# Chunks of 512 with spread preparation in a Mamba layer, and a second top-p attention whose search runs in three parts over three row tiles

## The chip, the cores and the metric

The kernel runs on one core of one Trainium2 chip. The metric is the device time of one execution in microseconds (us). All runs named here were in the fast state, and every kernel was timed beside the kernel before on the same chip. PE is TensorE, DVE is VectorE, ACT is ScalarE, POOL is GpSimd.

## The reference, cut to what matters

Four layers, each `x = layernorm(x + layer(x, adj))`, on x of 3327 rows (padded to 26 tiles of 128) by 256, fp32. The change touches layer 1 and layer 3.

```python
# layer 1: graph convolution, layer norm, Mamba (512 channels, 16 states)
h = relu(adj @ x @ gcn_w + gcn_b);  h = layernorm(h) * ln_g + ln_b
xc, z = split(h @ w_in)
u = silu(causal_conv4(xc));  dbc = u @ w_xp;  dt = softplus(dbc[:, :16] @ w_dt + b_dt)
B, C = dbc[:, 16:32], dbc[:, 32:]
hst[t] = exp(dt[t] * A) * hst[t-1] + dt[t] * B[t] * u[t]      # for each of 16 states
y = (hst @ C + u * D_skip) * silu(z);  out = y @ w_out

# layer 3: two steps; in each
probs = softmax((Xa @ W1.T @ W2.T) @ (Xa @ W3.T).T)
# keep the largest entries of a row until their sum reaches 0.9; equal entries by lower index first
A = probs * mask;  A = A / A.sum(-1)
Xf = R @ Xf;  Xa = A @ Xa;  Z = Z + Xf @ U1[n].T + Xa @ U2[n].T
```

In the first attention a row keeps few entries, in the second many. The second search therefore guesses a threshold c1, sums what lies over it, moves to c2, sums again, fits c3 a little below the cut, and ranks exactly only what lies under c3.

## The kernel before

Layer 1. `pump()` issues one step of the graph convolution's stream: six products, or the last two of a tile and its tail (nine products a step in the changed kernel). `head(c)` prepares a chunk of 384 columns, and all of it is issued after state 9 of the chunk before; `tail(c)` ends a chunk.

```python
            def head(c):

                w = min(WC, npad - c * WC)
                xc = scratch("xc")
                nc.vector.tensor_copy(xc[:, :, :3], last)
                u = ch.tile([P, NG, WC], F32, name="u")[:, :, :w]
                for g in range(NG):
                    nc.scalar.copy(xc[:, g, 3:3 + w], project(c, g, w))
                    ug = u[:, g, :]
                    nc.vector.tensor_scalar(ug, xc[:, g, 0:w], conv_w[:, g, 0:1], conv_b[:, g:g + 1],
                                            op0=ALU.mult, op1=ALU.add)
                    ...  # (three more taps; Silu of u; product with w_xp, copied to dbc: cut)
                e, e1 = scratch("e")[:, :, :w], scratch("e1")[:, :, :w]
                for g in range(NG):
                    ps = psum.tile([P, WC], F32, name="ps")
                    nc.tensor.matmul(ps[:, :w], w_dt[:, g * P:(g + 1) * P], dbc[:DTR, :w],
                                     start=True, stop=True)
                    nc.scalar.activation(dt[:, g, :], ps[:, :w], AF.Identity, bias=b_dt[:, g:g + 1])
                    nc.scalar.activation(e[:, g, :], ps[:, :w], AF.Abs, bias=b_dt[:, g:g + 1])
                nc.scalar.activation(e, e, AF.Exp, scale=-1.0)
                nc.vector.tensor_scalar_add(e1, e, 1.0)
                nc.vector.scalar_tensor_tensor(e, e1, 1.0, e, op0=ALU.subtract, op1=ALU.subtract)
                nc.scalar.activation(e1, e1, AF.Ln)
                nc.vector.tensor_sub(e1, e1, e)
                ...  # (dt = softplus, du = dt * u: cut)
                return u, dbc, dt, du

            def scan(dbc, dt, du, s, ys):
                ...
                for r in (DTR + s, DTR + DS + s):
                    ps = psum.tile([P, WC], F32, name="ps")
                    nc.tensor.matmul(ps[:, :w], ident[:R, r:r + 1].to_broadcast([R, P]), dbc[:, :w],
                                     start=True, stop=True)
                    row = work.tile([P, 1, WC], F32, name="row", bufs=4)
                    nc.scalar.copy(row[:, 0, :w], ps[:, :w])
                    bc.append(row[:, :, :w].to_broadcast([P, NG, w]))
                dA = work.tile([P, NG, WC], F32, name="dA", bufs=2)[:, :, :w]
                for g in range(NG):
                    nc.scalar.activation(dA[:, g, :], dt[:, g, :], AF.Exp, scale=A[:, g, s:s + 1])
                h = work.tile([P, NG, WC], F32, name="h")[:, :, :w]
                nc.vector.tensor_mul(h, du, bc[0])
                for g in range(NG):
                    nc.vector.tensor_tensor_scan(h[:, g, :], dA[:, g, :], h[:, g, :], initial=carry[:, s, g:g + 1],
                                                 op0=ALU.mult, op1=ALU.add)
                nc.vector.tensor_copy(carry[:, s, :], h[:, :, w - 1])
                nc.vector.tensor_mul(h, h, bc[1])
                for g in range(NG):
                    nc.tensor.matmul(ys[g][:, :w], ident, h[:, g, :], start=(s == 0), stop=(s == DS - 1))


            def tail(c, u, ys):

                w = u.shape[2]
                sz, y = scratch("sz")[:, :, :w], scratch("y")[:, :, :w]
                for g in range(NG):
                    nc.scalar.activation(sz[:, g, :], project(c, NG + g, w), AF.Silu)
                for g in range(NG):
                    nc.vector.scalar_tensor_tensor(y[:, g, :], u[:, g, :], d_skip[:, g:g + 1], ys[g][:, :w],
                                                   op0=ALU.mult, op1=ALU.add)
                nc.vector.tensor_mul(y, y, sz)
                nt_c = w // P
                ...  # (product with w_out, residual, layer norm of the chunk: cut)

            tw = WC // P
            pump(tiles=tw + 1)
            nxt = head(0)
            for c in range(nch):
                u, dbc, dt, du = nxt
                ys = [ypsum.tile([P, WC], F32, name=f"y{g}") for g in range(NG)]
                for s in range(DS):
                    scan(dbc, dt, du, s, ys)
                    pump()
                    if s == 9 and c + 1 < nch:
                        pump(tiles=(c + 2) * tw)
                        nxt = head(c + 1)
                tail(c, u, ys)
```

Layer 3. One tile's whole search comes before the attention of the tile before it:

```python
        def search_long(work, e, total, v, kept):
            nc.vector.max(m8, e)                                   # over all 3328 columns
            ...
            nc.scalar.activation(junk, e, AF.Exp, bias=hneg, scale=0.5, accum_out=root)
            exponentials(e, m8[:, 0:1], total)
            ...
            nc.scalar.activation(junk, e, AF.Sign, bias=c1, scale=-1.0, accum_out=sg)
            over(c1, m1)                  # DVE: sum of e where e >= c1
            ...  # k1 from sg; c2 from c1, k1, m1
            over(c2, m2)                  # DVE: sum of e where e >= c2
            ...  # c3 from c2 and the slope between the two sums
            nc.vector.scalar_tensor_tensor(z, e, c3, e, op0=ALU.is_lt, op1=ALU.mult, accum_out=rest)
            top = ranked(work, segment_tops(work, z), RPT)   # 32 segments of 104, top 8 each; 7 rounds
            cs = crossing(work, v, top, 8 * RPT, base, lim)
            ...  # rep: which copies of the value v are kept
            for k in range(0, TIES, 8):   # two replacements over 3328 columns
                nc.vector.match_replace(z, rep[:, k:k + 8], z if k else e, 2.0)
            nc.vector.scalar_tensor_tensor(e, z, v, e, op0=ALU.is_gt, op1=ALU.mult, accum_out=kept)

        # one_pass (es starts with the search of tile 0)
                for it in range(nt):
                    if it + 1 < nt:
                        es.append(ahead(it + 1))      # logits and search of the next tile
                    step(it, work, psum, atp, ...)    # attention of this tile, diffusion, finish
```

Of the kernel before, what the change touches and what calls it, by code (L numbers as in the profile page):

```python
# [22 lines left out]
JS = 6  # L23
WC = 384
# [9 lines left out]
SEG = 104  # L34
RP0, RPT = 6, 7
TIES = 16
UNDER = 24.0
KC = 416
# [3 lines left out]
def gnn_kernel(ctx: ExitStack, tc: tile.TileContext, n: int, a: dict, out: bass.AP):  # L42
# [84 lines left out]
    with tc.tile_pool(name="l01", bufs=1) as xpool:  # L127
# [30 lines left out]
        with tc.tile_pool(name="l1b", bufs=1) as wpool, tc.tile_pool(name="l1aw", bufs=2) as cwork, \  # L158
                tc.tile_pool(name="l1at", bufs=3) as atp, tc.tile_pool(name="l1c", bufs=2) as ch, \
                tc.tile_pool(name="l1t", bufs=4) as tmp, tc.tile_pool(name="l1s", bufs=3) as work, \  # L160
                tc.tile_pool(name="l1p", bufs=2, space=PSUM) as psum, \
# [26 lines left out]
            hTs = {}  # L188

            def scratch(name):  # L190
                return tmp.tile([P, NG, 3 + WC], F32, name="t")

            def convolve():

                for it in range(nt):
                    c, i = divmod(it * P, WC)
                    if i == 0:
                        hTs[c] = ch.tile([P, D // P, WC], F32, name="hT")
                    acc = cpsum.tile([P, D], F32, name="acc")
                    for j in range(nt):  # L200
# [5 lines left out]
                        if j % JS == JS - 1:  # L206
                            yield it
                    m = cwork.tile([P, D], F32, name="m")
                    nc.scalar.copy(m, acc)
                    mt = transposed(cwork, cpsum, m, "mt")  # L210
                    po = cpsum.tile([P, D], F32, name="acc")
                    for k in range(2):
                        nc.tensor.matmul(po, mt[:, k, :], gw[:, k, :], start=(k == 0), stop=False)
                    nc.tensor.matmul(po, one, gb, start=False, stop=True)
                    h = cwork.tile([P, D], F32, name="h")
                    nc.scalar.activation(h, po, AF.Relu)
# [5 lines left out]
                    pt = cpsum.tile([P, D // P, P], F32, name="ps")  # L222
                    for k in range(2):
                        nc.tensor.transpose(pt[:, k, :], h[:, k * P:(k + 1) * P], ident)
                        nc.scalar.activation(hTs[c][:, k, i:i + P], pt[:, k, :], AF.Identity,
                                             scale=g1[:, k:k + 1], bias=b1[:, k:k + 1])
                    yield it + 1
# [20 lines left out]
            def head(c):  # L248

                w = min(WC, npad - c * WC)  # L250
                xc = scratch("xc")
                nc.vector.tensor_copy(xc[:, :, :3], last)
                u = ch.tile([P, NG, WC], F32, name="u")[:, :, :w]
                for g in range(NG):
# [4 lines left out]
                    for k in range(1, 4):  # L259
                        nc.vector.scalar_tensor_tensor(ug, xc[:, g, k:k + w], conv_w[:, g, k:k + 1], ug,  # L260
                                                       op0=ALU.mult, op1=ALU.add)
                nc.vector.tensor_copy(last, xc[:, :, w:w + 3])
                nc.scalar.activation(u, u, AF.Silu)
                ps = psum.tile([P, WC], F32, name="ps")
# [4 lines left out]
                nc.scalar.copy(dbc[:, :w], ps[:R, :w])  # L269


                dt = ch.tile([P, NG, WC], F32, name="dt")[:, :, :w]
                e, e1 = scratch("e")[:, :, :w], scratch("e1")[:, :, :w]
                for g in range(NG):
# [3 lines left out]
                    nc.scalar.activation(dt[:, g, :], ps[:, :w], AF.Identity, bias=b_dt[:, g:g + 1])  # L278
                    nc.scalar.activation(e[:, g, :], ps[:, :w], AF.Abs, bias=b_dt[:, g:g + 1])
                nc.scalar.activation(e, e, AF.Exp, scale=-1.0)  # L280
                nc.vector.tensor_scalar_add(e1, e, 1.0)
                nc.vector.scalar_tensor_tensor(e, e1, 1.0, e, op0=ALU.subtract, op1=ALU.subtract)
                nc.scalar.activation(e1, e1, AF.Ln)
                nc.vector.tensor_sub(e1, e1, e)
                nc.vector.scalar_tensor_tensor(dt, dt, 0.0, e1, op0=ALU.max, op1=ALU.add)
                du = ch.tile([P, NG, WC], F32, name="du")[:, :, :w]
                nc.vector.tensor_mul(du, dt, u)
                return u, dbc, dt, du

            def scan(dbc, dt, du, s, ys):  # L290

                w = dt.shape[2]
                bc = []
                for r in (DTR + s, DTR + DS + s):
# [3 lines left out]
                    row = work.tile([P, 1, WC], F32, name="row", bufs=4)  # L298
                    nc.scalar.copy(row[:, 0, :w], ps[:, :w])  # L299
                    bc.append(row[:, :, :w].to_broadcast([P, NG, w]))  # L300
                dA = work.tile([P, NG, WC], F32, name="dA", bufs=2)[:, :, :w]
                for g in range(NG):
                    nc.scalar.activation(dA[:, g, :], dt[:, g, :], AF.Exp, scale=A[:, g, s:s + 1])  # L303
                h = work.tile([P, NG, WC], F32, name="h")[:, :, :w]
                nc.vector.tensor_mul(h, du, bc[0])  # L305
                for g in range(NG):
                    nc.vector.tensor_tensor_scan(h[:, g, :], dA[:, g, :], h[:, g, :], initial=carry[:, s, g:g + 1],  # L307
                                                 op0=ALU.mult, op1=ALU.add)
                nc.vector.tensor_copy(carry[:, s, :], h[:, :, w - 1])
                nc.vector.tensor_mul(h, h, bc[1])  # L310
                for g in range(NG):
                    nc.tensor.matmul(ys[g][:, :w], ident, h[:, g, :], start=(s == 0), stop=(s == DS - 1))  # L312

            def tail(c, u, ys):

                w = u.shape[2]
                sz, y = scratch("sz")[:, :, :w], scratch("y")[:, :, :w]
# [201 lines left out]
    with tc.tile_pool(name="l3", bufs=1) as pool, tc.tile_pool(name="l3s", bufs=4) as sm:  # L519
# [16 lines left out]
        for k in range(TIES):  # L536
            nc.vector.memset(count[:, k:k + 1], k)
# [402 lines left out]
```

## Time and profile before

| | us |
|---|---|
| median, 4 runs of the rounds with the changed kernel | 4768.2 (4766.3 to 4769.8) |
| layer 0 ends / layer 1 ends / layer 2 ends | 365 / 1942 / 2297 |
| first attention ends / second attention ends | 3240 / 4764 |

The span in 40 equal slices, from the page of the kernel before; a digit is the busy share in tenths, PEclk the granted clock of TensorE in tenths.

```profile
PE   8998888898888877899799999997577776767786
DVE  1111897788787888688245454541888888888886
PEclk9998998898898887999699999996788888888888
```

The two stretches where DVE shows mostly 7 or 8 and PE mostly 6 to 8 (slices 5 to 17 and 29 to 40) are layer 1 from its first scan on and the second attention. Where DVE shows 4 and 5 and PE 9, the kernel is TensorE's. The stretches, waits and groups that the argument rests on stand in the prediction.

### The profile page before, as it was taken

The numbers are of one execution on the slowest core, as the hardware profiler recorded it, in microseconds if no ns is written. First come the engines' busy times: TensorE is split into PE (matmuls) and PEld (weight loads), VectorE is DVE, ScalarE is ACT, GpSimd is POOL, SyncE is SP. The second block draws the span as 40 slices with busy tenths as digits, with TensorE's granted clock in tenths as the row PEclk, the third lists the DMA queues.
The fourth block names the chain that finished last, engine by engine and source line by source line (L and its number), as shares of the span: only waits on it lengthen the run. The fifth ranks groups of instructions, "written<-read, shape, count | busy, mean of one in ns | idle before, by whom it ended". The sixth has DMA issues, their size and how long they took to land. (4 is left out here: it accounts for less than half of the span.)

```text
span 4764.0 us, 44497 instructions
## 1 busy us (share of the span) xinstructions
PE 3980.5 (84%) x16077; PEld 2918.7 (61%) x16077; DVE 3173.4 (67%) x6838; ACT 1736.9 (36%) x3062; POOL 162.6 (3%) x162
## 2 busy tenths in 40 slices
PE   8998888898888877899799999997577776767786
PEld 7886545454454434688577777775455665656565
DVE  1111897788787888688245454541888888888886
ACT  0002545445444444300233333333334443444442
POOL 0000000000000000033000000000000000000000
PEclk9998998898898887999699999996788888888888
DMA  5433101110010000244011111110011111111110
GB/s 173 139 123 103 44 20 34 33 34 29 24 43 29 0 0 0 92 152 149 28 49 52 52 49 54 48 54 5 30 31 31 33 37 32 40 31 33 32 46 19
DMA packets 67063, 239.45 MB, mean 50 GB/s; under 512 B 8435, under 2 KB 22771, under 8 KB 66691
## 3 DMA queue, kind: packets, MB, share of 16 engines
q1 hardware_dynamic: 66818, 236.37, 15.5%
q8 instruction: 133, 2.18, 0.2%
q14 instruction: 112, 0.91, 0.1%
HBM read 232.93 MB, written 3.41 MB: 50 GB/s over the span
## 5 line engine op out<-in xcount | busy, mean ns | idle before, releaser
L312 PE MATMUL y<-h,ident 128*128 128x384 f32 (+1 forms) x1152 | 463.2, 550 | 123.2 <-DVE h L310 123.0
L307 DVE TENSOR_TENSOR_SCAN h<-dA,carry,h 128x384 f32<-128x384 f32 (+1 forms) x576 | 533.1, 974 | 1.0
L312 PEld LDWEIGHTS y<-h,ident 128*128 128x128 f32 x1152 | 239.8, 219 | 327.6 <-DVE h L310 194.8
L119 PE MATMUL ps<-ident,e 128*128 128x128 f32 x1352 | 204.7, 301 | 253.9 <-DVE e L714 215.3
L303 ACT ACTIVATE dA<-dt,A_log 128x384 f32<-128x384 f32 (+1 forms) x576 | 305.6, 593 | 261.4 <-DVE h L307 261.0
L119 PEld LDWEIGHTS ps<-ident,e 128*128 128x128 f32 x1352 | 176.5, 156 | 298.1 <-issue 269.5
L205 PE MATMUL acc<-X,at 128*128 128x256 f32 x1352 | 343.1, 401 | 17.6 <-DMA at<-in_adjT 12.4
L123 PE MATMUL acc<-Xa,wt 128*128 128x256 f32 x1352 | 341.1, 408 | 15.4 <-ACT wt L121 14.6
L296 PE MATMUL ps<-dbc,ident 48*128 48x384 f32 (+1 forms) x576 | 279.6, 599 | 61.4 <-ACT row L299 61.2
L123 PE MATMUL acc<-X,wt 128*128 128x256 f32 x1352 | 310.2, 383 | 21.5 <-ACT wt L121 19.5
L97 ACT COPY xt<-ps 128x256 f32<-128x256 f32 x234 | 83.1, 373 | 671.4 <-PE ps L95 640.8
L205 PEld LDWEIGHTS acc<-X,at 128*128 128x128 f32 x1352 | 259.4, 199 | 109.2 <-issue 54.1
L123 PEld LDWEIGHTS acc<-Xa,wt 128*128 128x128 f32 x1352 | 273.3, 207 | 67.1 <-ACT wt L121 26.9
L108 PE MATMUL acc<-xa,at 128*128 128x257 f32 x1352 | 308.0, 381 | 0.0
L108 PE MATMUL acc<-X,at 128*128 128x256 f32 x1352 | 304.3, 379 | 0.0
L121 ACT COPY wt<-ps 128x512 f32<-128x512 f32 (+1 forms) x364 | 188.3, 552 | 315.8 <-PE ps L119 312.4
L108 PE MATMUL acc<-Xf,at 128*128 128x256 f32 x1352 | 301.7, 379 | 0.0
L305 DVE TENSOR_TENSOR h<-du,row 128x1536 f32<-128x1536 f32 (+1 forms) x144 | 242.6, 1687 | 88.1 <-ACT row L299 82.2
L123 PEld LDWEIGHTS acc<-X,wt 128*128 128x128 f32 x1352 | 252.4, 190 | 70.3 <-ACT wt L121 38.0
L493 PE MATMUL acc<-V,at 128*128 128x257 f32 x1352 | 294.2, 379 | 1.1 <-DVE at L490 1.1
L584 PE MATMUL ps<-kT,q 64*128 64x416 f32 x832 | 255.7, 618 | 34.8 <-ACT q L570 25.8
L493 PEld LDWEIGHTS acc<-V,at 128*128 128x128 f32 x1352 | 255.8, 189 | 39.4 <-DVE at L490 1.4
(253 smaller groups left out, 6202.9 us busy)
## 6 DMA issues: line engine op xcount, KB each, us to landing
at<-in_adjT SPq DMA_DIRECT2D x156, 576.0 KB, 3.7
at<-in_adjT SPq DMA_DIRECT2D x104, 832.0 KB, 4.4
at<-in_adjT SPq DMA_DIRECT2D x78, 512.0 KB, 3.4
xa<-in_x SPq DMA_DIRECT2D x1, 3328.0 KB, 13.1
xt<-in_xT SPq DMA_DIRECT2D x26, 128.0 KB, 4.0
out<-h SPq DMA_DIRECT2D x25, 128.0 KB, 1.7
w_in<-in_w_in SPq DMA_DIRECT2D x1, 1024.0 KB, 5.3
U<-in_U SPq DMA_DIRECT2D x2, 512.0 KB, 6.4
```

The costliest lines, as they stand in the source:

```text
L108: nc.tensor.matmul(acc, at[:, j, :], rhs[:, j0 + j, :], start=(j0 + j == 0), stop=(j0 + j == nt - 1))
L119: nc.tensor.transpose(pt[:, j, :], w[:, (j0 + j) * P:(j0 + j + 1) * P], ident)
L121: nc.scalar.copy(wt[:, :m, :], pt[:, :m, :])
L123: nc.tensor.matmul(acc, wt[:, j, :], rhs[:, j0 + j, :], start=(j0 + j == 0), stop=(j0 + j == nt - 1))
L205: nc.tensor.matmul(acc, at[:, j % JC, :], X0[:, j, :], start=(j == 0), stop=(j == nt - 1))
L296: nc.tensor.matmul(ps[:, :w], ident[:R, r:r + 1].to_broadcast([R, P]), dbc[:, :w], start=True, stop=True)
L303: nc.scalar.activation(dA[:, g, :], dt[:, g, :], AF.Exp, scale=A[:, g, s:s + 1])
L305: nc.vector.tensor_mul(h, du, bc[0])
L307: nc.vector.tensor_tensor_scan(h[:, g, :], dA[:, g, :], h[:, g, :], initial=carry[:, s, g:g + 1], op0=ALU.mult, op1=ALU.add)
L312: nc.tensor.matmul(ys[g][:, :w], ident, h[:, g, :], start=(s == 0), stop=(s == DS - 1))
L493: nc.tensor.matmul(acc, at[:, j, :], V[:, j0 + j, :], start=(j0 + j == 0), stop=(j0 + j == nt - 1))
L584: nc.tensor.matmul(pl[:, :w], q[a:a + DA, :], kT[a:a + DA, c0:c0 + w], start=True, stop=True)
```

## The change

Its intent: take DVE's waits at the chunk borders out of layer 1 by laying the preparation of a chunk between the scans of the chunk before, with larger chunks; and in the second attention take the waits for the exponentials and some 12 us of work per row tile from DVE, by running the search in three parts on three different tiles, by moving one masked sum to ScalarE (a pass with Relu and one with Sign), and by shortening the passes (26 segments of 128, the first maximum over 416 columns, ties dropped by one replacement per half row, read backwards, so that the highest indices go first).

```diff
-JS = 6
-WC = 384
+WC = 512
...
-SEG = 104
-RP0, RPT = 6, 7
-TIES = 16
+SEG = 128
+RP0, RPT = 6, 6
... (layer 1: in the preparation `head(c)` a `yield` after each group of the convolution, after Silu, after dbc, dt, exponential;
     PSUM buffers for products 3 in place of 2, fewer of the other buffers; a tile's tail in two steps, its last transposes later)
+            def gate_input(c):
+                w = us[c].shape[2]
+                sz = szs[c] = ch.tile([P, NG, WC], F32, name="sz", bufs=1)[:, :, :w]
+                for g in range(NG):
+                    nc.scalar.activation(sz[:, g, :], project(c, NG + g, w), AF.Silu)
...
+            def gate(c, ys):
+                u = us[c]
+                w = u.shape[2]
                 for g in range(NG):
-                    nc.tensor.matmul(ys[g][:, :w], ident, h[:, g, :], start=(s == 0), stop=(s == DS - 1))
-
-            def tail(c, u, ys):
-
-                w = u.shape[2]
-                sz, y = scratch("sz")[:, :, :w], scratch("y")[:, :, :w]
-                for g in range(NG):
-                    nc.scalar.activation(sz[:, g, :], project(c, NG + g, w), AF.Silu)
-                for g in range(NG):
-                    nc.vector.scalar_tensor_tensor(y[:, g, :], u[:, g, :], d_skip[:, g:g + 1], ys[g][:, :w],
+                    nc.vector.scalar_tensor_tensor(u[:, g, :], u[:, g, :], d_skip[:, g:g + 1], ys[g][:, :w],
                                                    op0=ALU.mult, op1=ALU.add)
-                nc.vector.tensor_mul(y, y, sz)
-                nt_c = w // P
-                xo = cwork.tile([P, WC // P, D], F32, name="xo")
-                mv = small.tile([P, WC // P, 2], F32, name="mvc")
-                for i in range(nt_c):
+                nc.vector.tensor_mul(u, u, szs[c])
... (`back(c)`: the rest of the old `tail`)
-            nxt = head(0)
+            pump(tiles=tw)
+            x = None
+            for x in head(0):
+                pump()
+            pump(tiles=tw + 2)
+            nxt = rows(x, 0)
+            ys = None
             for c in range(nch):
-                u, dbc, dt, du = nxt
-                ys = [ypsum.tile([P, WC], F32, name=f"y{g}") for g in range(NG)]
+                w = us[c].shape[2]
+                ahead = None
                 for s in range(DS):
-                    scan(dbc, dt, du, s, ys)
+                    cur = nxt
+                    if s + 1 < DS:
+                        nxt = rows(x, s + 1)
+                    h = scan(x, s, *cur)
+                    if s == 0 and c:
+                        gate(c - 1, ys)
+                    if s == 0:
+                        ys = [ypsum.tile([P, WC], F32, name=f"y{g}") for g in range(NG)]
+                    for g in range(NG):
+                        nc.tensor.matmul(ys[g][:, :w], ident, h[:, g, :], start=(s == 0), stop=(s == DS - 1))
+                    if s == 0 and c:
+                        back(c - 1)
                     pump()
-                    if s == 9 and c + 1 < nch:
-                        pump(tiles=(c + 2) * tw)
-                        nxt = head(c + 1)
-                tail(c, u, ys)
+                    if s == DS - 10:
+                        gate_input(c)
+                    if s >= DS - 9 and c + 1 < nch:
+                        if ahead is None:
+                            pump(steps=0, tiles=(c + 2) * tw)
+                            ahead = head(c + 1)
+                        y = next(ahead)
+                if c + 1 < nch:
+                    x = y
+                    nxt = rows(x, 0)
+            gate(nch - 1, ys)
+            back(nch - 1)
```

Layer 3, the core of it:

```diff
+            e = logits(work, psum, xs, kT, it, 3)
-            nc.vector.max(m8, e)
+            nc.vector.max(m8, e[:, :KC])                       # KC = 416
...
+            yield None                                          # end of part 1 (exponentials)
             nc.scalar.activation(ajunk, e, AF.Sign, bias=c1, scale=-1.0, accum_out=sg)
             (masked sum m1, threshold c2)
-            over(c2, m2)
+            nc.vector.tensor_scalar_mul(nc2, c2, -1.0)
+            nc.scalar.activation(ajunk, e, AF.Relu, bias=nc2, accum_out=f2)
+            nc.scalar.activation(ajunk, e, AF.Sign, bias=c2, scale=-1.0, accum_out=sg)
+            yield None                                          # end of part 2
+            nc.vector.tensor_scalar(k2, sg, -0.5, npad / 2, op0=ALU.mult, op1=ALU.add)
+            nc.vector.scalar_tensor_tensor(m2, k2, c2, f2, op0=ALU.mult, op1=ALU.add)
...
-            for k in range(0, TIES, 8):
-                nc.vector.match_replace(z, rep[:, k:k + 8], z if k else e, 2.0)
-            nc.vector.scalar_tensor_tensor(e, z, v, e, op0=ALU.is_gt, op1=ALU.mult, accum_out=kept)
+            for r, c in ((r, half), (up, 0)):
+                ... (rep from r)
+                back = e[:, c:c + half][:, ::-1]
+                nc.vector.match_replace(back, rep, back, 0.0)
+            nc.vector.scalar_tensor_tensor(e, e, v, e, op0=ALU.is_ge, op1=ALU.mult, accum_out=kept)
+            yield e                                             # end of part 3
...
+                for i in range(-lead[0], nt):
+                    for part in lead:
+                        if 0 <= i + part < nt:
+                            es[i + part] = next(searches[i + part])
...
-        one_pass(Xa, search_long, second)
+        one_pass(Xa, search_long, second, (2, 1, 0))
```

Also, in layer 3's last step the reciprocal square roots come from POOL's power and not from ScalarE's square root, and scale and bias are merged into fewer DVE passes.

## The prediction

> **What bounds the kernel now.** I read the span in slices first, cut it into stages by the first and last instruction of each stage's lines, asked for the busy time of every engine in those stretches, then the waits of VectorE (DVE) in the two stretches that the change touches. The stages: layer 0 to 365 us, layer 1 (graph convolution and Mamba) to 1940, layer 2 to 2296, layer 3's first attention to 3241, its second attention to 4764. The stretches below are the steady parts; columns are PE, weight load, DVE, ACT and POOL busy us (instructions), granted clock, DMA share, GB/s.
>
> ```profile
> 487.00:1940.00 1453.00, 1219.90 (x3594) 687.70 (x3595) 1193.78 (x1397) 694.91 (x1252) 58.41 (x24) 0.88 0.08 24
> 1986.00:2296.00 310.00, 296.36 (x1363) 257.53 (x1362) 245.30 (x327) 23.81 (x58) 96.37 (x81) 0.98 0.44 151
> 2373.00:3241.00 868.00, 816.57 (x3962) 655.84 (x3958) 409.67 (x1534) 295.69 (x550) 2.28 (x23) 1.00 0.16 50
> 3379.00:4717.00 1338.00, 1007.02 (x4431) 800.76 (x4432) 1144.21 (x3038) 557.72 (x820) 2.28 (x23) 0.86 0.11 35
> ```
>
> Rows 2 and 3 are PE's own: PE busy 94 to 96%. Rows 1 and 4 have no engine above 86%: the time is DVE work plus waits of DVE. In row 1 DVE is idle 259 us, in row 4 194 us. The waits of DVE say on what, first in layer 1, then in the second attention:
>
> ```profile
> DVE h L305 <- ACT row L299: 82.2, 18, 14.2
> DVE xo L332 <- PE ps L330: 54.0, 22, 10.5
> DVE t L281 <- ACT t L280: 50.2, 4, 15.1
> DVE u L257 <- ACT t L255: 20.2, 6, 5.8
> ```
>
> ```profile
> DVE lim L622 <- ACT e L608: 81.6, 24, 3.9
> DVE c L651 <- ACT ajunk L643: 53.6, 16, 4.5
> DVE h L801 <- PE acc L799: 15.2, 14, 3.9
> DVE rs L74 <- ACT std L73: 12.7, 9, 2.2
> ```
>
> In layer 1 the waits sit at the borders of the nine 384-column chunks (few, up to 15 us each): the serial preparation of a chunk (projection, silu, softplus) and the tail of the last one. Inside a chunk, the timeline shows one state's step every 7.09 us with DVE never idle. In the second attention, DVE waits each row tile for the two exponentials (135 us, 5.4 per tile) and otherwise works. The costs that the change touches, from the groups by form:
>
> ```profile
> L307 DVE TENSOR_TENSOR_SCAN h<-dA,carry,h 128x384 f32<-128x384 f32 x512 | 489.5, 1003 | 1.0
> L305 DVE TENSOR_TENSOR h<-du,row 128x1536 f32<-128x1536 f32 x128 | 223.2, 1747 | 82.9 <-ACT row L299 82.2 <-PE y L312 0.6
> L658 DVE SCALAR_TENSOR_TENSOR djunk<-e,c 128x3328 bf16<-128x3328 f32 x52 | 191.5, 3684 | 1.8
> L638 DVE MAX8 m<-e 128x8 f32<-128x3328 f32 x26 | 93.7, 3603 | 76.2 <-ACT e L585 76.2
> L713 DVE MATCH_REPLACE8 z<-rep,z 128x3328 f32<-128x3328 f32 x26 | 93.8, 3608 | 0.0
> L73 ACT ACT_TABLE_LOAD x56 | 71.8, 1283 | 1.0
> ```
>
> [...] For 2048 I take 2282 (slope from the trace's own 1024-wide 1212). [...] the granted clock is 1.0 or 0.5 in pieces of 3.4 us, 1.00 in the first attention and 0.86 in the second. [...] The change reads and writes half a tile backwards[...].
>
> **Layer 1, part by part.** Chunks go from 384 to 512 columns (6.5 instead of 8.67), the preparation is cut into pieces laid after the scans of states 7 to 15, the tail goes behind the next chunk's first scan.
> - Scans: at 384, 7.09 us per state. At 512 the two products grow by 0.535 us each and the four scans by 0.267 (half-step of 1003 against 736 at 256): 9.29. Per 128 columns 2.32 instead of 2.36, over 26 tiles and 16 states 967 instead of 983 us: 16 us.
> - Preparation, tail and layer norms per 512 columns, from the forms at 256 and 384 carried on: convolution by taps 4 x (0.47 + 3 x 0.67) = 9.9, softplus 1.2 + 4 x 2.28 = 10.3, gate and output 8.4, four layer norms of 1.0; 32.6 in all, times 6.5, less the first chunk's 20 that lie before the first scan: about 190 us.
> - Sum of DVE: 967 + 190 = 1157, against 1194 measured busy. So nearly all the gain must come from the 259 us of waits. In the built order of after, the conv and softplus pieces stand between single scans, so a late one has a scan's 1.2 us and a step of slack before it. PE per full chunk, at 0.43 us per product of 256 columns (the chain of waits has 26 of them in 11.2 us): states 16 x 6 x 0.86 = 82, four tiles of convolution 4 x (11.2 + 2.1) = 53, projections and their like 20, output 7, in all 162 us, against 16 x 9.29 + 32.6 = 181 of DVE: 90%. An old steady step has the same share (six products of 384 and six of 256, 6.4 of 7.09 us), and the clock stayed at 1.0 through 133 us of them.
> - Against: six and a half tiles of convolution stand on PE before the first scan (four before), about +10 us[...].
> - I leave 45 of the 259 us of waits: 1157 + 45 + first scan at 500 + 15 for the end gives an end at 1715 to 1740 instead of 1940. **Gain 210 us.**
>
> **The second attention.** Per row tile, removed from DVE: the second masked sum (3.76, now two ScalarE passes of 3.08), the maximum over 3328 shrinks to 416 columns (-3.0), two replacements over 3328 become two over 1664 (-3.4), ranks on 208 instead of 256 candidates and one round fewer (-1.5), the segments (-0.4, since maxima follow each other every 0.17 us, not 0.25), finish and diffuse merged (-1.4); new small operations +1.2. So -12.3 from 45.8 busy (1144/25): 33.5 to 35 us. The square roots go to POOL, so ScalarE loses its table loads there.
>
> But the built order is not what the source reads like: on DVE the middle part of tile j directly follows the last pass of tile j-1, and the last part of j directly follows its middle. So DVE must wait within each tile for ScalarE's Relu and Sign (2 x 3.08 + 0.19 each, about 6.5 us with the handover). In return the attention of a tile runs a full tile later, and the exponentials come during the ranking of the tile before: the old 5.4 goes away. From one last pass to the next: to Relu's bias 6.4, Relu and Sign to 13.5, threshold 2, z 3.8, segments with finish in between 8.3, maximum 0.6, ranks 4.8, crossing 2.4, replacements 3.9, last pass 3.8: 43 us. PE's loop: a first-attention step takes 33.86 us by the timeline at full clock, finish adds 5.1 (eight products of 0.43, eight transposes of 0.21), and PE waits for the Sign of the next tile and for the diffused tile (about 5): 44 to 45. The two loops are nearly equal, so I take 45.5, against 1338/25 = 53.5. **Gain 25 x 8 = 200**, and some 8 in the fill and the final tile.
>
> First attention, layers 0 and 2: fewer segment maxima, but PE holds them; 0. Whether rows fall to the exact fallback I checked on the given inputs in fp32: no row in either kernel.
>
> Sum: 4768 - 210 - 208 = 4350; I go to 4365 for small handovers that I have not found.
>
> **Rivals.**
> 1. *The wait for Relu and Sign takes the place of the wait for the exponentials, and PE's loop binds*: for it, PE's 39 us per tile and the order; then a tile takes 48 to 50, the gain there is 90 to 140, and the time 4430.
> 2. *Backward replacement is slow*: [...]
> 3. *PE becomes layer 1's bound*: at clock 0.88 as now, 162 us become over 180, equal to DVE; then chunks take 200 us, layer 1 gains 120. Against it: the old steady steps had PE at 90% and clock 1.0.
> 4. *All waits vanish*: layer 1 ends at 1680, a tile takes 43, time 4270.
>
> **Range and chances.** Layer 1 +-60, second attention +-60, independent, gives about +-95. Both gains have to fail for less than 2% (95 us).
>
> **What would show each step.** Right: in layer 1 DVE busy near 1157, its waits below 80 us, states every 9.3 us, the first scan near 500. In the second attention DVE's largest wait is a small operation on the Sign sums, 5 to 7 us per tile; the wait on the exponentials is gone; period 44 to 47; no 1283 loads there; a half replacement 1.8 us. First attention still 868. Wrong if the half replacement takes over 3 us, if the maximum of 416 waits for all eight copies, or if DVE in layer 1 waits on PE.

## The result, and the profile after

The changed kernel took 4331.35 us (median of 4 runs, 4325.93 to 4335.09) against 4768.22: a ratio of 0.9083, 95% interval 0.9067 to 0.9099. A ratio is the mean time of one kernel's fast runs over that of the other's of the same rounds, so it is not quite the ratio of the medians quoted. By stages, from the first and last instruction of each stage's lines in both traces:

| stage | before, us | after, us | difference | predicted |
|---|---|---|---|---|
| layer 0 | 365 | 365 | 0 | 0 |
| layer 1 | 1577 | 1443 | -134 | -210 |
| layer 2 | 356 | 356 | 0 | 0 |
| first attention | 943 | 931 | -12 | 0 |
| second attention | 1523 | 1233 | -291 | -208 |

The span in 40 slices, the changed kernel:

```profile
PE   8998999999999977799889999999868889888988
DVE  1111588888888899688624444444158877787784
PEclk9998898989898988899969999999869999999999
```

PE now shows 9 through most of layer 1 and 8 or 9 in the second attention. DVE is denser than before in layer 1 (90% of the stretch below, 82% before) and thinner in the second attention (80%, before 86%). Busy times in layer 1, the first and the second attention of the changed kernel (columns as in the prediction):

```profile
500.00:1800.00 1300.00, 1151.53 (x3056) 592.48 (x3054) 1171.35 (x1116) 624.73 (x1011) 59.91 (x24) 0.89 0.08 26
2239.00:3096.00 857.00, 817.16 (x3961) 656.12 (x3960) 381.78 (x1360) 295.59 (x550) 24.39 (x47) 1.00 0.17 50
3222.00:4271.00 1049.00, 939.03 (x4352) 742.16 (x4353) 839.88 (x2832) 602.80 (x809) 81.28 (x167) 0.96 0.14 43
```

In layer 1 DVE works 1171 of 1300 us (90%) and PE 1152 (89%, at a clock of 0.89): neither is full. The first attention has the same PE work as before (817 us) in 11 us less. In the second, DVE works 33.6 us per tile (839.88/1049 of a period of 41.9) in place of 45.8.

DVE's waits of the changed kernel in layer 1 (500 to 1800), in total us, times, longest:

```profile
DVE db L336 <- ACT row L324: 82.6, 32, 6.7
DVE u L270 <- ACT t L268: 13.3, 10, 2.1
```

and in the second attention (3222 to 4271):

```profile
DVE k L750 <- ACT ajunk L748: 144.9, 24, 6.2
DVE nb L896 <- POOL rs L874: 18.7, 24, 1.1
DVE h L886 <- PE acc L884: 14.7, 24, 1.9
```

The row copy is ScalarE's copy of a row of B or C that TensorE has spread over all partitions. The border waits of layer 1 (up to 15 us each before) are gone, but a wait of 2.6 us on average for the row copies now comes 32 times. In total the waits for row copies are as long as before (82.6 against 82.2 us); what went are the others. In the second attention the wait for the exponentials is gone, and each of 24 tiles waits 6 us for Relu and Sign. Two groups by form of the changed kernel, with busy us and mean ns:

```profile
L788 DVE MATCH_REPLACE8 e<-rep,e 128x1664 f32<-128x1664 f32 x52 | 97.1, 1875 | 0.0
L708 DVE MAX8 m<-e 128x8 f32<-128x416 f32 x26 | 15.5, 595 | 70.8 <-ACT e L643 70.5
```

A backward replacement over half a row costs 1.88 us, just over half of the 3.61 of a forward one over the whole row (the difference is 1.04 ns for each column more, and so is that between forward ones over 208 and 3328 columns, 358 and 3608 ns): the step of -1 costs nothing here. The 70.8 us of idle time before the maximum are one wait of 69.3 us at the start of the stage; from 3222 on they are 1.4. The exact path for rows that the search cannot settle is in neither trace (no instruction of its bisection ran).

The time came as forecast in sum, but the two large parts missed in opposite directions, by 76 and 83 us. The experiments ask why.

### The profile page after: what moved, and what is told of

Same layout as the page of the kernel before. It is cut to its first block, busy times and chain, and to the rows that moved or that the text cites. A ratio compares the mean times of both kernels' runs of the same rounds, so it can differ in the third digit from the quotient of the medians.

```text
span 4327.9 us, 42860 instructions
## 1 busy us (share of the span) xinstructions
PE 3880.5 (90%) x15597; PEld 2791.7 (65%) x15597; DVE 2795.9 (65%) x6159; ACT 1731.7 (40%) x2826; POOL 276.6 (6%) x344
## 5 line engine op out<-in xcount | busy, mean ns | idle before, releaser
L393 PE MATMUL y<-h,ident 128*128 128x512 f32 (+1 forms) x896 | 466.4, 671 | 91.3 <-DVE h L342 91.3
L339 DVE TENSOR_TENSOR_SCAN h<-dA,carry,db 128x512 f32<-128x512 f32 (+1 forms) x448 | 511.6, 1193 | 4.8 <-DVE db L336 0.5
L328 ACT ACTIVATE dA<-dt,A_log 128x512 f32<-128x512 f32 (+1 forms) x448 | 281.4, 684 | 350.8 <-DVE h L339 333.1
L204 PE MATMUL cb<-X,at 128*128 128x256 f32 x1352 | 334.6, 403 | 26.9 <-ACT h L221 14.7
L204 PEld LDWEIGHTS cb<-X,at 128*128 128x128 f32 x1352 | 270.1, 203 | 113.7 <-issue 52.2
L107 PE MATMUL acc<-X,at 128*128 128x256 f32 x1352 | 304.3, 379 | 0.0
L336 DVE TENSOR_TENSOR db<-du,row 128x2048 f32<-128x2048 f32 (+1 forms) x112 | 238.9, 2133 | 82.8 <-ACT row L324 82.6
L107 PEld LDWEIGHTS acc<-xa,at 128*128 128x128 f32 x1352 | 255.6, 191 | 37.5 <-issue 0.7
L107 PEld LDWEIGHTS acc<-Xf,at 128*128 128x128 f32 x1352 | 251.4, 190 | 31.3
L321 PE MATMUL ps<-dbc,ident 48*128 48x512 f32 (+1 forms) x448 | 234.3, 637 | 20.3 <-ACT row L324 19.8
```

The costliest lines, as they stand in the source:

```text
L107: nc.tensor.matmul(acc, at[:, j, :], rhs[:, j0 + j, :], start=(j0 + j == 0), stop=(j0 + j == nt - 1))
L204: nc.tensor.matmul(acc, at[:, j % JC, :], X0[:, j, :], start=(j == 0), stop=(j == nt - 1))
L336: nc.vector.tensor_mul(db, du, bc[0])
L339: nc.vector.tensor_tensor_scan(h[:, g, :], dA[:, g, :], db[:, g, :], initial=carry[:, s, g:g + 1], op0=ALU.mult, op1=ALU.add)
```

## The experiments

The theory after reading the two traces: (a) in the second attention DVE's own chain, with the wait for Relu and Sign in it, sets the period of 41.9 us, and TensorE's loop, which the prediction put at 44 to 45 us, does not; (b) in layer 1 two regular places of each chunk cause the waits left: the block of four gate projections, and the block of four dt products. The main rivals: TensorE's loop binds the second attention; layer 1's waits come from table loads, or from TensorE as a whole. Summary, medians in us:

| run | kernel | median | kernel before, same rounds | ratio to it |
|---|---|---|---|---|
| | changed kernel | 4331.4 | 4768.2 | 0.9083 |
| e1 | layer 1 alone | 4631.5 | 4765.1 | 0.9719 |
| e2 | layer 3 alone | 4469.9 | 4765.1 | 0.9380 |
| e3 | search not spread | 4400.9 | 4765.1 | 0.9236 |
| e4 | second sum on DVE | 4255.8 | 4765.1 | 0.8933 |
| e5 | gate spread | 4338.5 | 4770.3 | 0.9099 |
| e6 | dt products in pairs | 4310.7 | 4770.3 | 0.9040 |
| e7 | power in layer 1 | 4341.8 | 4770.3 | 0.9106 |
| e8 | more TensorE work | 4351.8 | 4770.3 | 0.9114 |
| e9 | fewer products (wrong result) | 4772.9 | 4766.1 | 1.0015 |
| e10 | e4 and e6 | 4232.9 | 4766.1 | 0.8874 |
| e11 | e4, e5 and e6 | 4233.3 | 4766.1 | 0.8878 |
| e12 | maximum over full width | 4304.1 | 4763.8 | 0.9039 |

Stages that an edit did not touch differ by up to 7 us between builds (in e7, layer 2 and the first attention together against the changed kernel, for instance), so differences of that size are not read. No run was timed beside the changed kernel, and the kernel before took 4763.8 to 4770.3 us in the five sets of rounds. Against the changed kernel's 0.9067 to 0.9099, the 95% intervals of e5 (from 0.9086), e7 (from 0.9093) and e8 (from 0.9092) overlap, those of the runs that gained do not.

### e1 and e2: each half of the change alone

```diff
# e1: kernel before with the changed layer 1; e2: changed kernel with the old layer 1
-WC = 384          (e1)
+WC = 512
```

> The kernel before with the changed layer 1 alone (chunks of 512, spread preparation). Theory: the parts add up, so the whole 134 us that the two traces show for layer 1 appear here: 4768 - 134 = 4634 us (4622 to 4646), and the second attention keeps its 1523 us. Rival, the prediction's own sum: 210 us, 4558. Second rival: layer 1 gets shorter only together with the new layer 3 (through the buffers and the order of the whole program): less than 100 us, over 4668.

> The changed layer 3 with layer 1 of before. Theory: 291 us from the second attention and 12 from the first: 4768 - 303 = 4465 us (4453 to 4477), layer 1 ends near 1940. Rival, the prediction's sum for this part: 208 us, 4560.

Measured: 133.6 us for layer 1 (4765.1 to 4631.5) and 295.2 us for layer 3. Together 428.8 of the 436.9 us of the whole. The halves add up to within 8 us, and the sizes per stage are those of the traces. Both sums of the prediction are off, in opposite directions. Which part of layer 1's edit gained how much (the larger chunks, the spread preparation, the rows a state ahead, the buffers), no run separates.

### e3: the search not spread over three tiles

```diff
-        one_pass(Xa, search_long, second, (2, 1, 0))
+        one_pass(Xa, search_long, second, (1, 1, 1))
```

> The changed kernel, but the three parts of the second attention's search are taken from the same row tile, one tile ahead of its attention, as before, and not from three tiles. Everything else stays. Theory of the prediction: the spread removes the wait for the two exponentials, so it comes back: 5 to 6 us per tile, 25 tiles, 4331 + 125 to 150 = 4456 to 4481 us. Rival: the order that was built places the maximum of the next tile inside the present one in either case, so the spread alone is worth little: under 2 us per tile, 4331 to 4381.

Measured: 4400.9 us, 70 us over the changed kernel, 2.8 us per tile (from last pass to last pass 45.1 us in place of 41.9); it lies between the two theories. Some of DVE's waits in its second attention (3219 to 4348):

```profile
DVE k L750 <- ACT ajunk L748: 153.2, 24, 6.5
DVE lim L682 <- ACT e L713: 44.1, 24, 3.5
```

The wait for the exponentials comes back with 44.1 us, 1.8 per tile, a third of what it was before. So the spread is worth 70 us, but the wait for Relu and Sign is as large without it, 6.4 us per tile. As built, the middle part of a tile stands close before its last part on DVE in either case.

### e4: the second sum back on VectorE

```diff
-            nc.vector.tensor_scalar_mul(nc2, c2, -1.0)
-            nc.scalar.activation(ajunk, e, AF.Relu, bias=nc2, accum_out=f2)
-            nc.scalar.activation(ajunk, e, AF.Sign, bias=c2, scale=-1.0, accum_out=sg)
             yield None
-            (k2 and m2 from sg and f2)
+            nc.vector.scalar_tensor_tensor(djunk, e, c2, e, op0=ALU.is_ge, op1=ALU.mult, accum_out=m2)
```

> The changed kernel with the second masked sum back on VectorE, as one pass of about 3.7 us, in place of Relu and Sign on ScalarE for which VectorE waits 6.2 us per tile. If VectorE's own chain sets the period of 41.9 us: 2.5 us less per tile, 4331 - 62 = 4269 us (4255 to 4290). If TensorE's loop (rival 1) sets it: within 15 us of 4331. If instead ScalarE's relief counts too (6.1 us per tile less of it): up to 4 us per tile, 4231.

Measured: 4255.8 us, 75.6 us below the changed kernel, with a correct result, and at the lower edge of what was expected if VectorE's own chain sets the period. From last pass to last pass a tile now takes 38.65 us in place of 41.92. The stretch of its second attention:

```profile
3222.00:4189.00 967.00, 905.83 (x4316) 723.95 (x4317) 918.56 (x2788) 454.99 (x710) 85.95 (x167) 0.98 0.15 46
```

Its largest wait of DVE there:

```profile
DVE nb L892 <- POOL rs L870: 14.0, 24, 0.8
```

DVE works 3.1 us more per tile (918.56/967 of 38.65 is 36.7, against 33.6) and waits 5.8 us less (144.9/25). The net is 2.7 of the 3.3 us gained; the rest are smaller waits on PE. This shows that moving the second sum to ScalarE, which looks like relief for the busiest engine, cost 76 us, because DVE had nothing else in its order to do meanwhile. It also bounds TensorE's loop: it can do a tile in 38.65 us, not 44 (here without Relu and Sign on ScalarE, for whose copies TensorE waits: 18.7 us for those of the transposed weights in the changed kernel, 1.1 here). Now both engines are near full, DVE at 95% and PE at 94%.

### e8: more work on TensorE in the second attention

```diff
             vt = transposed(work, psum, v, "xt")
+            for k in range(8 if i == 0 else 0):      # overwritten by the next product's start
+                nc.tensor.matmul(pz, vt[:, 0, :], u[:, s, 0, :], start=True, stop=True)
```

> The changed kernel with eight more products of 256 columns (0.43 us each, 3.4 us of TensorE) per row tile in the last step of the second attention; their result is overwritten, so the output stays right. Theory: the period of 41.9 us is VectorE's chain, and TensorE has about 4.4 us of idle per tile: at most 1.5 us per tile, 4331 to 4369 us. Rival 1 of the prediction, TensorE's loop sets it: 3.4 us per tile, 25 tiles, 4331 + 86 = 4417 us.

Measured: 4351.8 us, 20 us more. Its second attention:

```profile
3222.00:4290.00 1068.00, 1008.74 (x4756) 811.75 (x4755) 846.89 (x2835) 602.91 (x809) 85.11 (x167) 0.98 0.14 43
```

PE is 70 us busier than in the changed kernel, and the period grew from 41.92 to 42.27 us, 0.35 us for 2.8 us of work per tile. The rest lies at the end: from the start of the last tile's last pass it is 75 us to the end of the kernel, in place of 61. TensorE does not set the period of the changed kernel. With e4, part (a) of the theory stands.

### e5: the gate's projections spread

In the changed kernel, one state of each full chunk looks so (timeline of PE; start and duration in us, operation, and in brackets the idle time before it and what ended it):

```profile
1002.04 7.03 PE L256 MATMUL ps<-hT,w_in 128*128 128x512 f32 x16
1009.00 1.98 PE L321 MATMUL ps<-dbc,ident 48*128 48x512 f32 x4
```

and so on DVE:

```profile
1010.78 2.29 DVE L336 TENSOR_TENSOR db<-du,row 128x2048 f32<-128x2048 f32 x1 [6.33 <-ACT row L324]
```

The trace lists each fp32 product as two instructions, half products here (26 x 26 products of the convolution are x1352). Sixteen half products of the gate stand on PE ahead of the row products, and DVE waits 6.33 us for the row. Spread them, and the wait should go:

```diff
-                    if s == DS - 10:
-                        gate_input(c)
+                    if 2 <= s < 2 + NG:
+                        gate_input(c, s - 2)          # one of the four projections
```

> The changed kernel; in layer 1 the four projections of the gate's input come one by one after the states 2 to 5 instead of all four after state 6. The trace of the changed kernel has, once per full chunk, a wait of 6.3 us of VectorE for the row copy while TensorE runs 16 half products of 7.0 us. Theory: this block ahead of the row product is the cause; without it about 5 to 6 us per chunk, six chunks, 4331 - 33 = 4298 us (4290 to 4310), and the total of VectorE's waits for the row copy falls from 83 to about 50 us. Rival: TensorE is layer 1's bound as a whole (prediction's rival 3), so its delay shows elsewhere: within 8 us of 4331. Three more pairs of table loads per chunk (2.6 us each) lie on ScalarE, which has room.

Measured: 4338.5 us, 7 more, none of the expected 33 gained. Layer 1 ends at 1814 in place of 1808. DVE's wait for the row copies between 500 and 1810:

```profile
DVE db L336 <- ACT row L324: 94.2, 40, 8.5
```

The one wait of 6.3 us per chunk and three of 0.8 to 1.7 before it became six of 1.3 to 3.4 us in six successive states, and the other one rose from 6.5 to between 7.4 and 8.5. The block stood in front of the row, as the timeline says, but taking it away gained nothing: the same work in other states makes DVE wait there. (The price of this spread, table loads of 1283 ns on ScalarE, is in it: 28 in place of 9 at the Silu of the gate, 53 in place of 39 at the exponentials of the states. ScalarE is 44 us busier between 500 and 1800, at 51%.) This miss changed the theory for layer 1: PE works its products off one after another in the built order, the sum of a state's work there (four y products, a convolution step, the rows, and in some states projections) is over DVE's 9.3 us in the busy states (3.70, 4.05, 1.98 and 7.03 us, together 16.8, in the state of the block above; 11.2 in a state of this run with one projection), and PE cannot use the idle time of the light states because its y products wait for DVE's h (91 us of waits of PE in layer 1).

### e6: the dt products in pairs

The second regular wait of a chunk in the changed kernel, in the timeline of PE (the last four dt half products, then the row products):

```profile
1095.67 2.72 PE L291 MATMUL ps<-dbc,w_dt 16*128 16x512 f32 x4
1098.32 3.78 PE L321 MATMUL ps<-dbc,ident 48*128 48x512 f32 x4
```

and what DVE does meanwhile:

```profile
1101.05 2.29 DVE L336 TENSOR_TENSOR db<-du,row 128x2048 f32<-128x2048 f32 x1 [6.49 <-ACT row L324]
```

Again DVE waits for a row behind a block on PE. The four row products take 3.78 us here and 1.98 us at the first place, about twice as long: the granted clock was 0.50 from 1098.3 to 1102 and 1.00 from 1009 to 1011. So besides the block the clock is a candidate for this wait.

```diff
                     nc.scalar.activation(e[:, g, :], ps[:, :w], AF.Abs, bias=b_dt[:, g:g + 1])
-                yield None
+                    if g % 2:
+                        yield None
...
-                    if s >= DS - 9 and c + 1 < nch:
+                    if s >= DS - 10 and c + 1 < nch:
```

> The changed kernel; in layer 1 the four products for dt, each with two ScalarE reads, come as two pairs after two different states (the preparation starts one state earlier) instead of four in a row. Theory: the second regular wait of a chunk, 6.5 us for the row copy, comes from these four holding the PSUM slots and ScalarE; halved or gone, 3 to 6 us in each of six chunks: 4331 - 27 = 4304 us (4293 to 4315). Rival, TensorE bounds layer 1: within 8 us of 4331.

Measured: 4310.7 us, 20.7 less by medians; layer 1 ends at 1780, 28 us earlier. DVE's wait for the row copies there (500 to 1810) fell from 82.6 to

```profile
DVE db L337 <- ACT row L325: 31.9, 15, 4.8
```

but a wait of 6.4 us for the copy of the first projection, once per chunk, came up (32.5 us in all). So the gain is there, at the lower end of what was expected, though the edit moves two things, the pairs and the start of the preparation one state earlier, which this run does not separate. Nor does any run separate the stretches at half clock: layer 1's mean granted clock is 0.90 here and 0.89 in the changed kernel.

### e7: power in place of square root in layer 1

```diff
-                    rstd_of(rs, mv[:, 1:2])
+                    pool_rstd(rs, mv[:, 1:2])      # POOL: add eps, then power -0.5
```

> The changed kernel; in layer 1 too the reciprocal square roots come from POOL's power, so that ScalarE changes its table less often (some 27 loads of 1.28 us go, and about as many for the way back to the exponential). Theory: these loads are beside the path but for the 6.7 us that VectorE waits for the square roots and a few us of late rows: 4331 - 10 = 4321 us (4311 to 4331). Rival: the loads delay the rows and are a main part of the 114 us of waits: more than 25 us gained, below 4306. Against a gain: the POOL operations have a handover of their own in each of the tiles.

Measured: 4341.8 us, 10 more. Layer 1 ends at 1809 against 1808. ScalarE is 63 us less busy in layer 1 (561.7 against 624.7; in the changed kernel 23 table loads of 1283 ns stand at the square roots there, and the exponentials of the states have 39, here 22), and no time is gained: DVE now waits for POOL in place of ScalarE, in layer 1 (500 to 1810):

```profile
DVE h L81 <- POOL rs L195: 33.4, 20, 5.1
```

DVE's waits for the row copies fell from 82.6 to 68.9 us, and its 6.7 us for the square roots went, so what the table loads can be seen to cost is some 20 us of layer 1's waits, not a main part. POOL's new waits took that back, and may hide more. The 10 us lie after layer 1 and are not explained; some 6 of them are in layer 2 and the first attention, within what builds differ by.

### e9: fewer products in the graph convolution

This kernel gives a wrong result on purpose.

```diff
+                        if j % JC not in (3, 4, 5):
                             nc.tensor.matmul(acc, at[:, j % JC, :], X0[:, j, :], ...)
```

> The changed kernel with a wrong result on purpose: in layer 1's graph convolution 9 of each tile's 26 products are left out (columns of the adjacency 3 to 5 of each nine), 3.9 us of TensorE per tile at full clock; VectorE and ScalarE keep all their work. Theory, formed after moving the gate brought nothing: the waits left in layer 1 come from TensorE's one queue, which holds in the busy half of a chunk more than VectorE's 9.3 us per state and cannot run ahead of it in the idle half. Then, beside some 25 us before the first scan, 40 to 80 us of the 114 us of waits go: 4331 - 65 to 105 = 4226 to 4266 us. Rival: the waits are latencies of ScalarE (row copies behind exponentials and table loads), which lighter TensorE work leaves alone: only the 25 us before the first scan, 4300 to 4310 us.

Measured: 4772.9 us, which says nothing: with the changed data one row tile in each attention went to the exact path (46 bisection steps in the trace, none in the changed kernel). Layer 1 can be read alone. It ends at 1741.5 in place of 1808.1, 66.6 us earlier: 16.3 before the first scan (493.4 in place of 509.7), not the 25 expected, and 50.3 inside. DVE's wait for the row copies fell from 82.6 us (500 to 1810) to (450 to 1700)

```profile
DVE db L337 <- ACT row L325: 41.4, 15, 5.2
```

So half of the waits for row copies, and a third of the time in which DVE does not work after the first scan begins (87 us in place of 131), come from the amount of PE's work. What makes the rest is not shown; the mean granted clock is still 0.88.

### e10 and e11: what gained, together

> Both changes that gained, together: the second sum back on VectorE (-75 us alone) and the dt products in pairs (-20 to -27 us alone). They lie in different stages, so they should add: 4331 - 98 = 4233 us (4220 to 4245). Rival: a gain in one shifts buffers or order in the other, over 4245.

> The one before, with the gate's projections also spread over the states 2 to 5. With the dt products in pairs the gate's block stands in the same state as the preparation's first projection, so spreading it may now help where it did not alone. Theory of TensorE's one queue: the states 2 to 5 have room only where no convolution step stands, so within 10 us of the kernel without it (about 4233). If the block itself were the cause: 30 us less, about 4200.

Measured: 4232.9 us for e10, the two edits of e4 and e6 together. It beats both kernels: 0.8874 of the kernel before, where the changed kernel had 0.9083. The gains add. e11 has the gate spread too, takes 4233.3, in line with e5: spreading the gate gains nothing that these runs can tell from zero.

### e12: the maximum over the full width

```diff
-            nc.vector.max(m8, e[:, :KC])
+            nc.vector.max(m8, e)
```

> The changed kernel with the first maximum of the second attention's search over all 3328 columns again, as before, instead of 416: 3.0 us more of VectorE per row tile (3.60 against 0.59). The result stays right. Theory: VectorE's chain is the period and this maximum stands in it, so 3.0 us per tile, 25 tiles, and a little in the fill: 4331 + 75 = 4406 us (4395 to 4415). Rival: the maximum slides into the 6.2 us in which VectorE waits for Relu and Sign, and costs under 1 us per tile, under 4356 us.

Measured: 4304.1 us, 27 less, where the theory said 75 more and the rival up to 25 more. Three more us of DVE work per tile made the kernel faster. The timeline of DVE over two tiles (masked sum of the middle part L725, first operation after Relu and Sign L750, last pass L789), in e12:

```profile
3787.57 3.68 DVE L725 SCALAR_TENSOR_TENSOR djunk<-e,c 128x3328 bf16<-128x3328 f32 x1
...
3797.41 3.67 DVE L789 SCALAR_TENSOR_TENSOR e<-e,v_all 128x3328 f32<-128x3328 f32 x1
...
3801.72 0.15 DVE L750 TENSOR_SCALAR k<-sg 128x1 f32<-128x1 f32 x1
...
3834.36 3.68 DVE L725 SCALAR_TENSOR_TENSOR djunk<-e,c 128x3328 bf16<-128x3328 f32 x1
...
3846.91 0.15 DVE L750 TENSOR_SCALAR k<-sg 128x1 f32<-128x1 f32 x1 [4.44 <-ACT ajunk L748]
```

and in the changed kernel:

```profile
3966.78 3.68 DVE L789 SCALAR_TENSOR_TENSOR e<-e,v_all 128x3328 f32<-128x3328 f32 x1
...
3970.64 3.68 DVE L725 SCALAR_TENSOR_TENSOR djunk<-e,c 128x3328 bf16<-128x3328 f32 x1
...
3982.82 0.15 DVE L750 TENSOR_SCALAR k<-sg 128x1 f32<-128x1 f32 x1 [6.24 <-ACT ajunk L748]
```

In the changed kernel the masked sum of a tile always follows the last pass of the tile before, so nothing lies between it and the wait but small operations. The longer maximum changed the order in which the instructions were placed when the kernel was built: in e12 the masked sum of every other tile stands ahead of the replacements and the last pass of the tile before (3787 before 3797), Relu and Sign run beside those 8 us, and L750 has no wait. Over the stretch (3222 to 4255) that wait falls from 144.9 us (24 times) to

```profile
DVE k L750 <- ACT ajunk L748: 51.5, 13, 4.4
```

DVE's busy time rises by 68, and the period goes from 41.92 to 40.68 us. Some 26 of the 27 us lie in the second attention. So the wait for Relu and Sign is a matter of order. What an order with every tile so would bring, no run shows. What the 416 columns are worth by themselves is also left open, since the edit could not be made without moving the order.

## Why the prediction was right or wrong

**The total.** 4331 us lies in the range and 34 us under the forecast, but by luck: an overestimate of layer 1's gain and an underestimate of layer 3's cancelled, and each part missed its own +-60. The verdict was safe either way: layer 3 alone (e2) gives 0.938.

**Layer 1.** The DVE work was right (1157 forecast, 1170 measured from 507 to 1808), and so was the first scan (500, measured 507). The step that failed is "I leave 45 of the 259 us of waits". With the 15 us for the end that is 60 us of DVE not working after the first scan; measured are 131 (1301 less 1170). So the layer gained some 128 us of waits (259 to 131) and 24 of work (1194 to 1170), less 20 for the later first scan (487 to 507). The two products over 2048 columns, for which the forecast carried the times of the trace at 1024 and 1536 (1212 and 1747 ns) on to 2282, took 2286 and 2289 ns. The sum was loose as well: 7.09 + 2 x 0.535 + 4 x 0.267 is 9.23 and not 9.29 us per state (6 us over the layer), and 1157 + 45 + 500 + 15 is 1717, of which 1715 to 1740 was made; both are small beside the miss. The reason given, that "a late one has a scan's 1.2 us and a step of slack before it", looked at the preparation and not at the rows, which are what DVE waits for (82.6 of the 131 us, as many as before the change). A state took 13.0 us on average over a full chunk, not the 11.3 that 181 us per chunk are. Rival 3 named the right engine and nearly the size (chunks of 200 us and a gain of 120; measured 208 and 134), and its "against", that steady steps before had PE at 90% and clock 1.0, does not carry over: the clock was 0.89. But PE is not a plain bound; e9 takes some 100 us of its full-clock work in the layer away (26 tiles of 3.9 us) and gains 67. The order of the products, with both engines at 90%, is the reading that fits e5, e6 and e9; no run isolates it, or the half clock, for the rest. Part (b) of the later theory fell in half: spreading the gate's block brought nothing (e5, e11), cutting the dt block with an earlier start gained 28 us in the layer (e6).

**Second attention.** The list of DVE work removed was right to about 1 us per tile (33.5 to 35 forecast, 33.6 measured), and the chain of 43 us close to the measured 41.9. The wait foreseen on the Sign sums, "about 6.5 us with the handover", measured 6.0 as a mean (144.9/24). The step that failed is "PE's loop: ... 44 to 45" and the 45.5 taken from it. It started from the first attention's period of 33.86 us, which already has PE's own waits in it (868 less 817 us over the stretch, some 2 us per tile), and added 5 us of waits to finish. e4 shows that the loop fits in 38.65 us once Relu and Sign are off ScalarE, e8 that PE has room in the changed kernel. Of the 3.6 us per tile between 45.5 and 41.9, 2.5 are this surcharge and 1.1 the chain: 90 us over 25 tiles, against which the 8 us for fill and final tile came out near 2.

**First attention.** Forecast 0, measured 12 us less. PE's wait for the copies of the transposed weights fell from 19.5 to 8.7 us, which is nearly all of it. Why the copies come earlier was not tested.

**The rivals.** Rival 1 fell in its second half: the wait for Relu and Sign did take the place of the wait for the exponentials, but it is DVE's wait and PE's loop does not bind. Rival 2 fell: a half replacement takes 1.88 us (that a backward one is slow, no trace had shown). Rival 4 came nowhere near in layer 1, but its 43 us per tile were the nearest of all for the second attention (41.9). Of the signs, DVE's work in layer 1, the first scan, the wait on the Sign sums, the half replacement and the absence of table loads in the second attention (none from 3222 to 4271) came true; layer 1's waits below 80 us, the period of 44 to 47 and the unchanged 868 did not (131, 41.9 and 857). In layer 1 DVE waited 14 us on PE itself and 83 on the row copies that stand behind PE's products.

**What was not seen.** The forecast noted that the built order "is not what the source reads like", and then took that order as given. It is where the next gain was: moving the sum back (e4) gave 76 us, and an accident of order (e12) 27.

## What to carry to other kernels

Before work is moved from the busiest engine to an idle one, ask whether the busy engine has something to do in its own order until the result is back; here 3.7 us of own work beat 6 us of waiting (e4, 76 us). When two engines are both near 90% in a stretch, as here DVE and PE in layer 1 (90 and 89%), do not forecast that the waits go: ask what each state holds in the fuller queue, and expect a wait to move when one block is moved (in e5 one of 6.3 us became six of 1.3 to 3.4). When the built order is not the source's, a change of one instruction's length can reorder a whole loop (e12, a maximum of 3.60 us in place of 0.59), so compare orders before reading a slope experiment.

## Instruction times that the runs show

- VectorE: 1875 ns for a replacement over 1664 fp32 columns read and written backwards (forwards 358 ns over 208 and 3608 over 3328), and for the maximum 278 ns over 128 columns, 378 over 208, 595 over 416 and 3603 over 3328.
- POOL: for a power over 128x1 a median of 567 ns in e7's layer 1, and means of 583 ns in layer 3 and 691 ns in layer 2 of the changed kernel; for the addition before it in e7's layer 1 a mean of 799 ns. VectorE waited 1.7 us on average for the result there (33.4 us, 20 times), against 6.7 us in 5 waits for ScalarE's square root, with its table load of 1283 ns, in the changed kernel.
